# A recommender's attention block: feeding the label's term through eight extra contraction rows in place of a seeded PSUM tile, with label rows gathered by index in place of single-row copies

## The chip, the cores and the metric

The kernel runs on one core of a Trainium2 chip. The metric is the device time of one execution in microseconds (us); the time given is the median of three executions. The profile is one execution recorded by the hardware profiler. In it PE is TensorE's products, PEld its weight loads, DVE is VectorE, ACT is ScalarE, POOL is GpSimd and SP is the SyncE queue, which here only issues DMAs. A name such as L229 is a line of the kernel's file.

## The reference, cut to what matters

For each of 16384 samples there are 69 item ids and one label id. All are rows of one embedding table of 100001 rows of 96 floats. Each item's embedding u meets the label's embedding q in a small attention network; the attended embeddings are summed in ten groups of fields, and three dense layers follow.

```python
u  = emb[batch_user]                     # [B, 69, 96]
ql = emb[batch_label[:, 0]]              # [B, 96]
q  = broadcast of ql over the 69 fields
z  = concatenate([q, u, q - u, q * u], axis=-1)      # [B, 69, 384]
h  = dice(z @ W1 + b1, a1)               # [B, 69, 64], dice(x) = (a (1-p) + p) x, p = sigmoid(x)
att = (h @ W2 + b2) @ W3 + b3            # [B, 69, 1]
pre = where(batch_user < ITEM_NUM, u * att, 0)
pooled = einsum('gf,bfe->bge', window, pre)          # ten groups of fields
x = concatenate([pooled, ql])            # 1056 wide
# three dense layers (200, 80, 1), the first two with batch norm and dice
```

With W1 cut into four pieces of 96 rows, `z @ W1 + b1` is the sum of three terms: `q (W1a + W1c) + b1`, which depends on the sample alone and is called **c** here; `u (W1b - W1c)`, whose weight is called A; and `(q*u) W1d`, whose weight is called Wp. The change is about how c gets into the sum.

## The kernel before

Samples are taken in 32 blocks of 512. A block has 69 chunks of 512 (sample, field) places: 64 chunks hold eight samples with their first 64 fields each, and five tail chunks hold one field of all 512 samples. Chunks are worked on in pairs, 1104 in all; in PSUM the two chunks of a pair lie side by side, the first on partitions 0 to 63, the second on 64 to 127.

The item rows of a chunk come in by four gathers of 128 rows from GpSimd, into one of 14 `u` tiles; TensorE transposes them, VectorE multiplies by q, ScalarE copies the transposed rows:

```python
def gather(dst, index):
    nc.gpsimd.indirect_dma_start(out=dst, out_offset=None, in_=emb,
        in_offset=bass.IndirectOffsetOnAxis(ap=index, axis=0))          # L229

def fetch(i):
    u = upool.tile([P, 8, E], F32, tag="u", name=f"u{i}")                # 14 buffers
    uT, quT = ...                                                        # 5 buffers each
    for j in range(2):
        n, k = chunk(2 * i + j)
        ptr = ps_tr.tile([E, 512], F32, tag="tr", name=f"ptr{i}_{j}")
        for t in range(4):
            gather(u[:, 4 * j + t, :], rows[n][:, 4 * k + t : 4 * k + t + 1])
            nc.tensor.transpose(ptr[:, t * P : (t + 1) * P], u[:, 4 * j + t, :], ident)   # L325
        # VectorE: quT = ptr * q (q broadcast over the 64 fields, or as it is in a tail chunk)   L328, L335
        nc.scalar.copy(uT[:, j, :], ptr)                                 # L336
```

The label rows of block 0 come in by four such gathers. Those of all other blocks are fetched row by row: SP loads 32 labels into registers and issues 32 DMAs of one row each, sixteen times for a block:

```python
def head_gather(n, part):
    ...
    for i, row in enumerate(at):
        nc.sync.dma_start(out=qs[n][p + i : p + i + 1, k, :], in_=emb[bass.ds(row, 1), :])   # L260
```

c is worked out for a whole block, in two layouts (cT with the second half shifted by eight samples, cU without). For each pair a `seed` opens the PSUM tile with a product of zeros, so that later products add to it, and ScalarE writes c over it; `hidden` then adds the two products:

```python
def seed(i):
    ph = ps_h.tile([P, 512], F32, tag="h", name=f"ph{i}")
    nc.tensor.matmul(ph, zrow[:, 0:P], zrow, start=True, stop=False)     # L295, one bf16 row
    # ScalarE copies c into ph: cT spread over 64 fields (L298), cU in tail chunks (L302),
    # or half by half in pairs that mix the two (L307, L312)
    return ph

def hidden(i, ph, uT, quT):
    for w, x, last in [(A, uT, False), (Wp, quT, True)]:
        for j in range(2):
            nc.tensor.matmul(ph[j * H1 : (j + 1) * H1, :], w, x[:, j, :], start=False, stop=last)   # L343
    # sigmoid (L345), scale (L346), product with ph (L347) -> y
```

Further on, four y tiles give a row of attention values (L354, L356), which is turned (L370) and multiplied with the group table (`rw`, L376), and `pool` sums the attended rows into groups (L393, L402). Tail chunks go through L363 and L364, and the dense layers through L423 to L449.

The program is written as a loop over pairs, in which step i seeds pair i-1, pools pair i-8, runs `hidden` for pair i-2 and fetches pair i. A plan hangs the work of block n on the steps near `first`, the pair at which the block begins:

```python
at(first - 24, load ids of block n)         # SP
at(first - 21, map ids to table rows)       # VectorE
at(first - 31 + part, head_gather(n, part)) # part 0 to 15
at(first - 11, head_turn(n))                # transposes q into qT
at(first - 9,  head_row(n))                 # c of the block
at(end + 8 + 4 + s, dense layers of block n, ten steps)   # the last one stores the output from SP
```

Of the kernel before, what the change touches and what calls it, by code (L numbers as in the profile page):

```python
# [28 lines left out]
F32 = mybir.dt.float32  # L31
BF16 = mybir.dt.bfloat16
I32 = mybir.dt.int32
AF = mybir.ActivationFunctionType
ALU = mybir.AluOpType
PSUM = bass.MemoryType.PSUM

P = 128
# [8 lines left out]
FM = 64  # L47
NTAIL = F - FM
NS = BLK // FM
NMAIN = BLK // NS  # L50
NCH = NMAIN + NTAIL
NQ = BLK // P
NT = NCH * 4
NCOL = NT + NQ
NLD = 32
NPAIR = NBLK * NCH // 2
# [8 lines left out]
def rec_kernel(  # L65
    ctx: ExitStack,
    tc: tile.TileContext,
    idx: bass.AP,
    lab: bass.AP,
    emb: bass.AP,  # L70
# [23 lines left out]
    upool = ctx.enter_context(tc.tile_pool(name="upool", bufs=14))  # L94
    tpool = ctx.enter_context(tc.tile_pool(name="tpool", bufs=5))
    hpool = ctx.enter_context(tc.tile_pool(name="hpool", bufs=3))
# [10 lines left out]
    def map_ids(n, ids):  # L107

        rows = ipool.tile([P, NT], I32, tag="rows", name=f"rows{n}")
        nc.vector.scalar_tensor_tensor(rows, ids[:, 0:NT], float(ITEM_NUM), ids[:, 0:NT], ALU.is_ge, ALU.add)  # L110
        return rows

    ids, rows = {0: load_ids(0)}, {}
# [7 lines left out]
    nc.sync.dma_start(out=w1, in_=W1.rearrange("(k e) h -> e k h", e=E))  # L121
    Cq = const.tile([E + 1, 2, H1], F32, name="Cq")
    for i in range(2):
        nc.vector.tensor_add(Cq[0:E, i, :], w1[:, 0, :], w1[:, 2, :])
    nc.sync.dma_start(
        out=Cq[E : E + 1], in_=b1.rearrange("(o q h) -> o q h", o=1, q=1).to_broadcast([1, 2, H1])
    )
    Wp = w1[:, 3, :]
    A = const.tile([E, H1], F32, name="A")
    nc.vector.tensor_sub(A, w1[:, 1, :], w1[:, 2, :])  # L130

    qTs = []
    for i in range(2):
        t = const.tile([E + 1, BLK + NS], F32, name=f"qT{i}")
        nc.vector.memset(t[:, BLK:], 0.0)
        nc.vector.memset(t[E : E + 1, :], 1.0)
        qTs.append(t)
# [60 lines left out]

    zrow = const.tile([1, 512], BF16, name="zrow")
    nc.vector.memset(zrow, 0.0)  # L200

    with tc.tile_pool(name="prep_ps", bufs=1, space=PSUM) as pps:
# [33 lines left out]
    def chunk(c):  # L236

        return divmod(c, NCH)

    def first_head():  # L240

        q = bpool.tile([P, NQ, E], F32, tag="q", name="q0")
        for k in range(NQ):
            gather(q[:, k, :], ids[0][:, NT + k : NT + k + 1])
        return q

    def head_gather(n, part):

        if part == 0:
            qs[n] = bpool.tile([P, NQ, E], F32, tag="q", name=f"q{n}")  # L250
        k, p = divmod(part * NLD, P)
        _, at = nc.values_load_multi_w_load_instructions(  # L252
            lab[n : n + 1, part * NLD : (part + 1) * NLD],
            engines=[mybir.EngineType.SP],
            min_val=0,
            max_val=ITEM_NUM,
            skip_runtime_bounds_check_because="labels are rows of the table",
        )
        for i, row in enumerate(at):
            nc.sync.dma_start(out=qs[n][p + i : p + i + 1, k, :], in_=emb[bass.ds(row, 1), :])  # L260

# [5 lines left out]

    def head_row(n):

        cT = bpool.tile([P, BLK], F32, tag="cT", name=f"cT{n}")  # L270
        pc = ps_x.tile([P, BLK], F32, tag="x", name=f"pc{n}")
        for i in range(2):
            nc.tensor.matmul(
                pc[i * H1 : (i + 1) * H1, :],
                Cq[:, i, :],
                qTs[n % 2][:, i * NS : i * NS + BLK],
                start=True,
                stop=True,
            )
        nc.scalar.copy(cT, pc)  # L280

        cU = bpool.tile([P, BLK], F32, tag="cU", name=f"cU{n}")
        pc = ps_x.tile([P, BLK], F32, tag="x", name=f"pc2_{n}")
        nc.tensor.matmul(pc, Cq.rearrange("e i h -> e (i h)"), qTs[n % 2][:, 0:BLK], start=True, stop=True)
        nc.scalar.copy(cU, pc)
        return cT, cU

    def by_field(ap):

        return ap.rearrange("e (s o) -> e s o", o=1).to_broadcast([ap.shape[0], NS, FM])  # L290

    def seed(i):

        ph = ps_h.tile([P, 512], F32, tag="h", name=f"ph{i}")
        nc.tensor.matmul(ph, zrow[:, 0:P], zrow, start=True, stop=False)  # L295
        (n0, k0), (n1, k1) = chunk(2 * i), chunk(2 * i + 1)
        if n0 == n1 and k1 < NMAIN:
            nc.scalar.copy(  # L298
                ph.rearrange("h (s f) -> h s f", f=FM), by_field(cs[n0][0][:, k0 * NS : (k0 + 1) * NS])
            )  # L300
        elif n0 == n1 and k0 >= NMAIN:
            nc.scalar.copy(ph, cs[n0][1])  # L302
        else:
            for j, (n, k) in enumerate([(n0, k0), (n1, k1)]):
                lo, hi = j * H1, (j + 1) * H1
                if k < NMAIN:
                    nc.scalar.copy(  # L307
                        ph[lo:hi].rearrange("h (s f) -> h s f", f=FM),
                        by_field(cs[n][1][lo:hi, k * NS : (k + 1) * NS]),
                    )  # L310
                else:
                    nc.scalar.copy(ph[lo:hi], cs[n][1][lo:hi, :])  # L312
        return ph

    def fetch(i):

        u = upool.tile([P, 8, E], F32, tag="u", name=f"u{i}")
        uT = tpool.tile([E, 2, 512], F32, tag="uT", name=f"uT{i}")
        quT = tpool.tile([E, 2, 512], F32, tag="quT", name=f"quT{i}")
        for j in range(2):  # L320
            n, k = chunk(2 * i + j)
# [4 lines that stand above are left out]
            q = qTs[n % 2][0:E]  # L326
            if k < NMAIN:
                nc.vector.tensor_tensor(  # L328
                    quT[:, j, :].rearrange("e (s f) -> e s f", f=FM),
                    ptr.rearrange("e (s f) -> e s f", f=FM),  # L330
                    by_field(q[:, k * NS : (k + 1) * NS]),
                    ALU.mult,
                )
            else:
                nc.vector.tensor_tensor(quT[:, j, :], ptr, q[:, 0:BLK], ALU.mult)  # L335
            nc.scalar.copy(uT[:, j, :], ptr)  # L336
        return u, uT, quT

    def hidden(i, ph, uT, quT):

        for w, x, last in [(A, uT, False), (Wp, quT, True)]:
            for j in range(2):
                nc.tensor.matmul(ph[j * H1 : (j + 1) * H1, :], w, x[:, j, :], start=False, stop=last)  # L343
        y = ypool.tile([P, 512], F32, tag="y", name=f"y{i}")
        nc.scalar.activation(y, ph, AF.Sigmoid, scale=S_DICE)  # L345
        nc.scalar.activation(y, y, AF.Identity, bias=a1c, scale=na1c)  # L346
        nc.vector.tensor_mul(y, ph, y)  # L347
        return y
# [10 lines left out]
    def attend_tail(i, j, y, uT):  # L359
# [3 lines left out]
        nc.tensor.matmul(pa, vrep[j * H1 : (j + 1) * H1, :], y[j * H1 : (j + 1) * H1, :], start=True, stop=True)  # L363
        nc.vector.scalar_tensor_tensor(pres[n][:, k - NMAIN, :], pa, bb[0:E], uT[:, j, :], ALU.add, ALU.mult)  # L364

# [78 lines left out]
    def top3(n, x2):  # L444
        p3 = ps_m.tile([1, BLK], F32, tag="m", name=f"p3_{n}")
        nc.tensor.matmul(p3, wf3, x2, start=True, stop=True)
        res = xpool.tile([1, BLK], F32, tag="res", name=f"res{n}")
        nc.vector.tensor_scalar(res, p3, bf3c, None, ALU.add)
# [3 lines left out]

    cs, pooled, pres, x1s, x2s, qs, us, hs, phs, ys, bands, rws, p1s = ({} for _ in range(13))

# [19 lines left out]
    for n in range(NBLK):  # L474
        first, end = n * NCH // 2, ((n + 1) * NCH - 1) // 2
        if n > 0:
            at(first - 24, lambda n=n: ids.__setitem__(n, load_ids(n)))
            at(first - 21, lambda n=n: rows.__setitem__(n, map_ids(n, ids[n])))
            for part in range(BLK // NLD):
                at(first - 31 + part, lambda n=n, part=part: head_gather(n, part))  # L480
            at(first - 11, lambda n=n: head_turn(n, qs.pop(n)))
            at(first - 9, lambda n=n: cs.__setitem__(n, head_row(n)))
        for s, work in enumerate(top_steps(n)):
# [4 lines left out]
    with tc.manual_schedule():  # L488
        head_turn(0, first_head())
        cs[0] = head_row(0)  # L490
        for i in range(NPAIR + POOL_LAG + 16):
            if 0 <= i - 1 < NPAIR:
                phs[i - 1] = seed(i - 1)
            if 0 <= i - POOL_LAG < NPAIR:
# [18 lines left out]
            if 0 <= i - 2 < NPAIR:  # L513
                ys[i - 2] = hidden(i - 2, phs.pop(i - 2), *hs[i - 2])
            if i < NPAIR:
# [58 lines left out]
```

## Time and profile before

| | before |
|---|---|
| time, median of 3 (us) | 11180.09 (11178.86 to 11183.8) |
| span of the profiled execution (us) | 11177.1 |
| mean granted TensorE clock | 0.707 |
| gathers of item rows (POOL, L229) | 8832, mean 951 ns |
| single-row label DMAs (SP, L260) | 15872, 0.4 KB each |
| product of zeros (PE, L295) | 1104, mean 478 ns |
| seeding copies (ACT, L298) | 1008, mean 587 ns |
| DMA traffic | 456.81 MB, mean 41 GB/s |

The page gives for each engine the time in which it executed, as a share of the span. For POOL, the time of an instruction is that of issuing the gather, not of the rows' arrival. A group of instructions is written as line, engine, operation, output and inputs; behind the first bar stand its busy time and the mean of one, behind the second the time the engine was idle just before these instructions, and what ended most of it. "issue" means that the profile shows nothing that the engine waited for.

### The profile page before, as it was taken

What the parts mean: (1) busy time and instruction counts of PE and PEld (TensorE: products, weight loads), DVE (VectorE), ACT (ScalarE), POOL (GpSimd) and SP (SyncE); (2) the same over time, 40 slices, a digit from 0 to 9 for tenths busy, and PEclk for the clock granted to TensorE, in tenths of its full rate; (3) what the DMA queues carried; (4) which work ended last, traced back from release to release, by engine and by line L of the source; (5) the groups of instructions that cost most, each with busy time, mean ns of one, the idle gap of its engine ahead of it and who ended that gap; (6) DMA issues with size and microseconds to landing.
All of it is one profiled execution on the core that took longest, in us unless ns stands there. A gap on an engine that the chain in (4) does not pass through costs nothing.

```text
span 11177.1 us, 157529 instructions
## 1 busy us (share of the span) xinstructions
PE 9700.5 (87%) x41348; PEld 4721.0 (42%) x41348; DVE 3187.3 (29%) x5424; ACT 3760.0 (34%) x6086; POOL 8404.8 (75%) x8842
## 2 busy tenths in 40 slices
PE   6888888888888898888888888888888888988888
PEld 3444444444444444444444444444444344444444
DVE  2222222222222222222222222222222222222222
ACT  2333333333333333333333333333333333333332
POOL 7777777777777777777777777777777777777775
PEclk6767677677776767767777667776677776677767
DMA  2222222222222222222222222222222222222221
GB/s 45 41 41 41 41 41 41 41 41 41 41 41 41 41 41 41 41 42 41 41 41 41 41 41 41 40 41 42 41 41 41 41 42 41 41 41 41 41 40 29
DMA packets 323169, 456.81 MB, mean 41 GB/s; under 512 B 175712, under 2 KB 180864, under 8 KB 322272
## 3 DMA queue, kind: packets, MB, share of 16 engines
q0 software_dynamic: 282752, 434.87, 19.6%
q1 hardware_dynamic: 37886, 10.92, 0.5%
q8 instruction: 333, 5.46, 0.2%
q14 instruction: 564, 4.62, 0.1%
q10 hardware_dynamic: 1634, 0.94, 0.0%
HBM read 446.04 MB, written 0.07 MB: 40 GB/s over the span
## 4 chain that ended last, share of the span: by engine, by line
PE 33%; POOL 32%; issue 16%; DMA 10%; SPq 5%; ACT 2%; DVE 1%; POOLq 0%; ACTq 0%
POOL u L229 32%; PE ph L343 12%; DMA u<-in_emb,rows 10%; PE acc L393 9%; PE p L423 4%; SPq L260 3%; PE ptr L325 3%; PE prow L354 2%; SPq L252 2%; PE ph L295 2%; PE pa L363 1%; ACT y L346 1%; DVE y L347 1%; ACT y L345 1%; PE patt L370 1%
## 5 line engine op out<-in xcount | busy, mean ns | idle before, releaser
L229 POOL DMA_INDIRECT u<-in_emb,rows x8832 | 8400.1, 951 | 2692.9 <-issue 2459.0
L325 PE MATMUL ptr<-ident,u 128*96 128x128 f32 x8832 | 2006.4, 353 | 1189.5 <-DMA u<-in_emb,rows 1172.1
L325 PEld LDWEIGHTS ptr<-ident,u 128*96 128x96 f32 x8832 | 1221.0, 155 | 3053.7 <-DMA u<-in_emb,rows 1526.9
L393 PEld LDWEIGHTS acc<-rw,u 128*96 128x96 f32 x16384 | 2048.5, 217 | 531.8 <-issue 531.2
L393 PE MATMUL acc<-rw,u 128*96 128x20 f32 x16384 | 2160.4, 282 | 1.8 <-DVE rw L376 1.3
L336 ACT COPY uT<-ptr 96x512 f32<-96x512 f32 x2208 | 1283.4, 581 | 2207.0 <-DVE quT L328 2039.4
L347 DVE TENSOR_TENSOR y<-ph,y 128x512 f32<-128x512 f32 x1104 | 763.5, 692 | 4394.8 <-ACT y L346 4292.3
L345 ACT ACTIVATE y<-ph 128x512 f32<-128x512 f32 x1104 | 659.1, 597 | 3754.1 <-PE ph L343 3753.9
L343 PE MATMUL ph<-uT,A 96*64 96x512 f32 x4416 | 1793.5, 904 | 0.0
L343 PE MATMUL ph<-quT,w 96*64 96x512 f32 x4416 | 1671.9, 847 | 0.0
L328 DVE TENSOR_TENSOR quT<-ptr,qT 96x512 f32<-96x512 f32 x2048 | 1348.9, 679 | 611.5 <-PE ptr L325 607.0
L402 DVE COPY pooled<-acc 96x160 f32<-96x160 f32 x1008 | 433.3, 430 | 2189.9 <-PE acc L393 2184.4
L346 ACT ACTIVATE y<-y,a1c,na1c 128x512 f32<-128x512 f32 x1104 | 897.2, 813 | 36.6
L343 PEld LDWEIGHTS ph<-quT,w 96*64 96x64 f32 x4416 | 442.8, 194 | 1074.9 <-issue 1074.9
L298 ACT COPY ph<-cT 128x512 f32<-128x512 f32 x1008 | 591.3, 587 | 498.2 <-PE ph L295 497.8
L295 PE MATMUL ph<-zrow 1*128 1x512 bf16 x1104 | 527.6, 478 | 193.4 <-DVE y L347 191.7
L423 PE MATMUL p<-pooled,wf 96*100 96x512 f32 x1280 | 659.4, 660 | 1.2 <-DVE x L427 0.8
L343 PEld LDWEIGHTS ph<-uT,A 96*64 96x64 f32 x4416 | 282.6, 177 | 550.0 <-issue 464.8
L354 PE MATMUL prow<-y,v 128*32 128x512 f32 x2208 | 455.2, 909 | 0.0
L356 ACT COPY row<-prow 128x512 f32<-128x512 f32 x276 | 161.5, 585 | 628.4 <-PE prow L354 622.9
L423 PEld LDWEIGHTS p<-pooled,wf 96*100 96x100 f32 x1280 | 232.2, 190 | 287.7 <-issue 285.5
L423 PE MATMUL p<-pre,V 96*100 96x512 f32 x640 | 314.6, 625 | 0.0
(71 smaller groups left out, 2318.5 us busy)
## 6 DMA issues: line engine op xcount, KB each, us to landing
q<-in_emb SPq DMA_DIRECT2D x15872, 0.4 KB
u<-in_emb,rows POOLq DMA_INDIRECT x8832
ids<-in_idx SPq DMA_DIRECT2D x32, 140.0 KB
wf<-in_Wf ACTq DMA_DIRECT2D x1, 825.0 KB
out<-res SPq DMA_DIRECT2D x32, 2.0 KB
w<-in_W SPq DMA_DIRECT2D x1, 96.0 KB
q<-in_emb,ids POOLq DMA_INDIRECT x4
wf<-in_Wf ACTq DMA_DIRECT2D x1, 62.5 KB
```

What stands on the lines that cost most here:

```text
L229: nc.gpsimd.indirect_dma_start(out=dst, out_offset=None, in_=emb, in_offset=bass.IndirectOffsetOnAxis(ap=index, axis=0),)
L295: nc.tensor.matmul(ph, zrow[:, 0:P], zrow, start=True, stop=False)
L325: nc.tensor.transpose(ptr[:, t * P : (t + 1) * P], u[:, 4 * j + t, :], ident)
L328: nc.vector.tensor_tensor(quT[:, j, :].rearrange("e (s f) -> e s f", f=FM), ptr.rearrange("e (s f) -> e s f", f=FM), by_field(q[:, k * NS ...
L336: nc.scalar.copy(uT[:, j, :], ptr)
L343: nc.tensor.matmul(ph[j * H1 : (j + 1) * H1, :], w, x[:, j, :], start=False, stop=last)
L345: nc.scalar.activation(y, ph, AF.Sigmoid, scale=S_DICE)
L346: nc.scalar.activation(y, y, AF.Identity, bias=a1c, scale=na1c)
L347: nc.vector.tensor_mul(y, ph, y)
L354: nc.tensor.matmul(pr[32 * k : 32 * (k + 1), :], v2, y, start=True, stop=True)
L393: nc.tensor.matmul(pa[:, j, 2 * t : 2 * t + 2, :].rearrange("e n g -> e (n g)"), u[:, 4 * j + t, :], rw[:, i % 4, j, t, :], start=True, st ...
L423: nc.tensor.matmul(p1, w[:, h * DH : (h + 1) * DH], x, start=(k == 0), stop=(k == KTOP - 1))
```

## The change

c is no longer written into PSUM. The contraction of the first product grows from 96 rows to 104: the moving operand gets eight constant rows that say which of the chunk's eight samples a column belongs to, and the weights get the eight samples' rows of c below A. There are then 64 weight tiles (one for each chunk of a block), held in two tiles of 32, and the rows of c are put there by small DMAs from SP. In tail chunks, where each column is another sample, c comes from a product of its own with Cq. The product of zeros and the seeding copies go away.

The label rows of every block are gathered by GpSimd with four gathers, as block 0's were; the single-row DMAs of SP go away. The gathers stand at first - 14. The mapped ids are written in place, the uT tiles become five constant tiles, quT has four buffers in place of five, and the output row shares a buffer with another tile.

What it is for: to take the opening product and the copies off TensorE and ScalarE.

The diff, with the removed bodies of `seed`, `head_row` and the old `head_gather` (all shown above) and small declarations cut:

```diff
     def map_ids(n, ids):
-        rows = ipool.tile([P, NT], I32, tag="rows", name=f"rows{n}")
-        nc.vector.scalar_tensor_tensor(rows, ids[:, 0:NT], float(ITEM_NUM), ids[:, 0:NT], ALU.is_ge, ALU.add)
+        rows = ids[:, 0:NT]
+        nc.vector.scalar_tensor_tensor(rows, rows, float(ITEM_NUM), rows, ALU.is_ge, ALU.add)
         return rows
 ...
-    A = const.tile([E, H1], F32, name="A")
-    nc.vector.tensor_sub(A, w1[:, 1, :], w1[:, 2, :])
+    A = [const.tile([E + NS, HM, H1], F32, name=f"A{h}") for h in range(2)]
+    nc.vector.tensor_sub(A[0][0:E, 0, :], w1[:, 1, :], w1[:, 2, :])
+    for h in range(2):
+        nc.vector.tensor_copy(
+            A[h][0:E, 1 - h :, :], A[0][0:E, 0:1, :].to_broadcast([E, HM - 1 + h, H1])
+        )
+    uTs = [const.tile([E + NS, 2, 512], F32, name=f"uT{i}") for i in range(5)]
+    for t in uTs:
+        for j in range(2):
+            nc.vector.tensor_copy(
+                t[E : E + NS, j, :].rearrange("e (s f) -> e s f", f=FM), by_field(ident[E : E + NS, E : E + NS])
+            )
 ...
+    def head_gather(n):
+        q = bpool.tile([P, NQ, E], F32, tag="q", name=f"q{n}")
         for k in range(NQ):
-            gather(q[:, k, :], ids[0][:, NT + k : NT + k + 1])
+            gather(q[:, k, :], ids[n][:, NT + k : NT + k + 1])
         return q
 ...
+    def head_rows(n):
+        c = bpool.tile([P, NQ, H1], F32, tag="c", name=f"c{n}")
+        pc = ps_x.tile([P, NQ, H1], F32, tag="x", name=f"pc{n}")
+        for k in range(NQ):
+            nc.tensor.matmul(pc[:, k, :], qTs[n % 2][:, k * P : (k + 1) * P], Cq, start=True, stop=True)
+        nc.scalar.copy(c, pc)
+        return c
+
+    def head_weights(c, h):
+        for s in range(NS):
+            for k in range(NQ // 2):
+                nc.sync.dma_start(
+                    out=A[h][E + s : E + s + 1, k * HM // 2 : (k + 1) * HM // 2, :],
+                    in_=c[s::NS, h * NQ // 2 + k, :],
+                )
 ...
-    def hidden(i, ph, uT, quT):
-        for w, x, last in [(A, uT, False), (Wp, quT, True)]:
-            for j in range(2):
-                nc.tensor.matmul(ph[j * H1 : (j + 1) * H1, :], w, x[:, j, :], start=False, stop=last)
+    def hidden(i, uT, quT):
+        ph = ps_h.tile([P, 512], F32, tag="h", name=f"ph{i}")
+        places = [chunk(2 * i + j) for j in range(2)]
+        sums = [ph[j * H1 : (j + 1) * H1, :] for j in range(2)]
+        for (n, k), p in zip(places, sums):
+            if k >= NMAIN:
+                nc.tensor.matmul(p, Cq, qTs[n % 2], start=True, stop=False)
+        for j, ((n, k), p) in enumerate(zip(places, sums)):
+            if k < NMAIN:
+                nc.tensor.matmul(p, A[k // HM][:, k % HM, :], uT[:, j, :], start=True, stop=False)
+            else:
+                nc.tensor.matmul(p, A[0][0:E, 0, :], uT[0:E, j, :], start=False, stop=False)
+        for j, p in enumerate(sums):
+            nc.tensor.matmul(p, Wp, quT[:, j, :], start=False, stop=True)
 ...
-            for part in range(BLK // NLD):
-                at(first - 31 + part, lambda n=n, part=part: head_gather(n, part))
+            at(first - 14, lambda n=n: qs.__setitem__(n, head_gather(n)))
             at(first - 11, lambda n=n: head_turn(n, qs.pop(n)))
-            at(first - 9, lambda n=n: cs.__setitem__(n, head_row(n)))
+            at(first - 9, lambda n=n: cs.__setitem__(n, head_rows(n)))
+            at(first - 7, lambda n=n: head_weights(cs[n], 0))
+            at(first + 4, lambda n=n: head_weights(cs.pop(n), 1))
```

More of the change, by code (lines that the diff above doesn't have):

```diff
@@ L31 @@
 F32 = mybir.dt.float32
-BF16 = mybir.dt.bfloat16
 I32 = mybir.dt.int32
@@ L50 @@
 NMAIN = BLK // NS
+HM = NMAIN // 2
 NCH = NMAIN + NTAIL
@@ L54 @@
 NCOL = NT + NQ
-NLD = 32
 NPAIR = NBLK * NCH // 2
@@ L68, in rec_kernel @@
     idx: bass.AP,
-    lab: bass.AP,
     emb: bass.AP,
@@ L94, in rec_kernel @@
     upool = ctx.enter_context(tc.tile_pool(name="upool", bufs=14))
-    tpool = ctx.enter_context(tc.tile_pool(name="tpool", bufs=5))
+    tpool = ctx.enter_context(tc.tile_pool(name="tpool", bufs=4))
     hpool = ctx.enter_context(tc.tile_pool(name="hpool", bufs=3))
@@ L107, in map_ids, with by_field @@
     def map_ids(n, ids):
-        rows = ipool.tile([P, NT], I32, tag="rows", name=f"rows{n}")
-        nc.vector.scalar_tensor_tensor(rows, ids[:, 0:NT], float(ITEM_NUM), ids[:, 0:NT], ALU.is_ge, ALU.add)
-        return rows
+        rows = ids[:, 0:NT]
+        nc.vector.scalar_tensor_tensor(rows, rows, float(ITEM_NUM), rows, ALU.is_ge, ALU.add)
+        return rows
+    def by_field(ap):
+        return ap.rearrange("e (s o) -> e s o", o=1).to_broadcast([ap.shape[0], NS, FM])
     ids, rows = {0: load_ids(0)}, {}
@@ L121, in rec_kernel @@
     nc.sync.dma_start(out=w1, in_=W1.rearrange("(k e) h -> e k h", e=E))
[L122 to L127, printed above, removed]
-    Wp = w1[:, 3, :]
-    A = const.tile([E, H1], F32, name="A")
-    nc.vector.tensor_sub(A, w1[:, 1, :], w1[:, 2, :])
+    Cq = const.tile([E + 1, H1], F32, name="Cq")
+    nc.vector.tensor_add(Cq[0:E], w1[:, 0, :], w1[:, 2, :])
+    nc.sync.dma_start(out=Cq[E : E + 1], in_=b1.rearrange("(o h) -> o h", o=1))
+    Wp = w1[:, 3, :]
+    A = [const.tile([E + NS, HM, H1], F32, name=f"A{h}") for h in range(2)]
[10 more added lines that the diff above has]
+            )
     qTs = []
     for i in range(2):
-        t = const.tile([E + 1, BLK + NS], F32, name=f"qT{i}")
-        nc.vector.memset(t[:, BLK:], 0.0)
+        t = const.tile([E + 1, BLK], F32, name=f"qT{i}")
         nc.vector.memset(t[E : E + 1, :], 1.0)
@@ L197, in rec_kernel @@
     nc.vector.tensor_scalar_mul(sbf2, bf2c, S_BN)
-    zrow = const.tile([1, 512], BF16, name="zrow")
-    nc.vector.memset(zrow, 0.0)
     with tc.tile_pool(name="prep_ps", bufs=1, space=PSUM) as pps:
@@ L238, in chunk @@
         return divmod(c, NCH)
-    def first_head():
-        q = bpool.tile([P, NQ, E], F32, tag="q", name="q0")
+    def head_gather(n):
+        q = bpool.tile([P, NQ, E], F32, tag="q", name=f"q{n}")
         for k in range(NQ):
-            gather(q[:, k, :], ids[0][:, NT + k : NT + k + 1])
+            gather(q[:, k, :], ids[n][:, NT + k : NT + k + 1])
         return q
[L247 to L260, printed above, removed]
     def head_turn(n, q):
@@ L266, in head_turn @@
         nc.vector.tensor_copy(qTs[n % 2][0:E, 0:BLK], pq)
[L268 to L313, printed above, removed]
+    def head_rows(n):
[5 more added lines that the diff above has]
+        return c
@@ L315, in fetch @@
+    def head_weights(c, h):
[5 more added lines that the diff above has]
+                )
     def fetch(i):
         u = upool.tile([P, 8, E], F32, tag="u", name=f"u{i}")
-        uT = tpool.tile([E, 2, 512], F32, tag="uT", name=f"uT{i}")
+        uT = uTs[i % len(uTs)]
         quT = tpool.tile([E, 2, 512], F32, tag="quT", name=f"quT{i}")
@@ L335, in fetch @@
                 nc.vector.tensor_tensor(quT[:, j, :], ptr, q[:, 0:BLK], ALU.mult)
-            nc.scalar.copy(uT[:, j, :], ptr)
+            nc.scalar.copy(uT[0:E, j, :], ptr)
         return u, uT, quT
-    def hidden(i, ph, uT, quT):
-        for w, x, last in [(A, uT, False), (Wp, quT, True)]:
-            for j in range(2):
-                nc.tensor.matmul(ph[j * H1 : (j + 1) * H1, :], w, x[:, j, :], start=False, stop=last)
+    def hidden(i, uT, quT):
[12 more added lines that the diff above has]
+            nc.tensor.matmul(p, Wp, quT[:, j, :], start=False, stop=True)
         y = ypool.tile([P, 512], F32, tag="y", name=f"y{i}")
@@ L363, in attend_tail @@
         nc.tensor.matmul(pa, vrep[j * H1 : (j + 1) * H1, :], y[j * H1 : (j + 1) * H1, :], start=True, stop=True)
-        nc.vector.scalar_tensor_tensor(pres[n][:, k - NMAIN, :], pa, bb[0:E], uT[:, j, :], ALU.add, ALU.mult)
+        nc.vector.scalar_tensor_tensor(pres[n][:, k - NMAIN, :], pa, bb[0:E], uT[0:E, j, :], ALU.add, ALU.mult)
     def spread(b, row):
@@ L446, in top3 @@
         nc.tensor.matmul(p3, wf3, x2, start=True, stop=True)
-        res = xpool.tile([1, BLK], F32, tag="res", name=f"res{n}")
+        res = xpool.tile([DH, BLK], F32, tag="g1", name=f"res{n}")[0:1]
         nc.vector.tensor_scalar(res, p3, bf3c, None, ALU.add)
@@ L451, in rec_kernel @@
     out_v = out.rearrange("(n b) o -> n (o b)", n=NBLK)
-    cs, pooled, pres, x1s, x2s, qs, us, hs, phs, ys, bands, rws, p1s = ({} for _ in range(13))
+    cs, pooled, pres, x1s, x2s, qs, us, hs, ys, bands, rws, p1s = ({} for _ in range(12))
     def top_steps(n):
@@ L488, in rec_kernel @@
     with tc.manual_schedule():
-        head_turn(0, first_head())
-        cs[0] = head_row(0)
+        qs[0] = head_gather(0)
+        head_turn(0, qs.pop(0))
+        cs[0] = head_rows(0)
+        for h in range(2):
+            head_weights(cs[0], h)
         for i in range(NPAIR + POOL_LAG + 16):
-            if 0 <= i - 1 < NPAIR:
-                phs[i - 1] = seed(i - 1)
             if 0 <= i - POOL_LAG < NPAIR:
@@ L513, in rec_kernel @@
             if 0 <= i - 2 < NPAIR:
-                ys[i - 2] = hidden(i - 2, phs.pop(i - 2), *hs[i - 2])
+                ys[i - 2] = hidden(i - 2, *hs[i - 2])
             if i < NPAIR:
@@ L535 @@
     tail = user[:, :, FM:].reshape(NBLK, NQ, P, NTAIL).transpose(0, 2, 3, 1).reshape(NBLK, P, NTAIL * NQ)
+    labels = x["batch_label"].reshape(NBLK, NQ, P).transpose(0, 2, 1)
     window = x["window"]
@@ L539 @@
         wtile[n, :, n, :] = window[:, :FM].T
-    labels = x["batch_label"].reshape(NBLK, NQ, P).transpose(0, 2, 1)
     arrays = {
         "idx": np.concatenate([main, tail, labels], axis=2),
-        "lab": x["batch_label"].reshape(NBLK, BLK),
         "emb": np.concatenate([x["emb"], np.zeros((1, E), np.float32)], axis=0),
```

## The prediction

> **What bounds the kernel now.** I read four views in this order: the page's busy shares, the view of the gather's source line, the waits, and the timeline around single gathers.
>
> The busy shares alone mislead. TensorE is the busiest engine and GpSimd, which issues the gathers, seems to have a quarter of the span to spare:
>
> ```profile
> PE 9700.5 (87%) x41348; PEld 4721.0 (42%) x41348; DVE 3187.3 (29%) x5424; ACT 3760.0 (34%) x6086; POOL 8404.8 (75%) x8842
> ```
>
> The view of the source line that gathers gives duration (least, median, greatest, in ns) and the first and last start:
>
> ```profile
> L229 POOL DMA_INDIRECT u<-in_emb,rows x8832: 940/944/1582, 8.6 to 11100.4; - x197
> ```
>
> The waits say what the missing quarter is (after the arrow: what ended the idle time, then the microseconds in all, the times, the longest single one):
>
> ```profile
> POOL u L229 <- issue: 2459.0, 8065, 0.3
> ...
> POOL u L229 <- PE ptr L325: 105.8, 347, 0.3
> POOL u L229 <- DMA u<-in_emb,rows: 101.9, 334, 0.3
> ```
>
> Every one of the 8832 gathers is preceded by about 0.3 us of idle time, and the longest is 0.3 us too, whichever engine is put down as the releaser. So GpSimd never waits for anybody: 0.3 us is the price of starting a gather, and one named after PE or DMA is the same gap with an event near it. Listing all gathers from the timeline, I find no gap over 0.32 us. The first gather starts at 8.6 us and the last at 11100.4, so the period is (11100.4 - 8.6) / 8831 = **1.256 us**, and the time is a sum of three pieces: 8.6 us of head, 8831 x 1.256 = 11091.8 us of gathers, 76.7 us of tail after the last gather starts. That is the whole span of 11177.1.
>
> The groups by cost say the same from TensorE's side (columns: busy us, mean ns | idle us before, and what ended it):
>
> ```profile
> L229 POOL DMA_INDIRECT u<-in_emb,rows x8832 | 8400.1, 951 | 2692.9 <-issue 2459.0
> L325 PE MATMUL ptr<-ident,u 128*96 128x128 f32 x8832 | 2006.4, 353 | 1189.5 <-DMA u<-in_emb,rows 1172.1
> ...
> L343 PE MATMUL ph<-uT,A 96*64 96x512 f32 x4416 | 1793.5, 904 | 0.0
> ...
> L298 ACT COPY ph<-cT 128x512 f32<-128x512 f32 x1008 | 591.3, 587 | 498.2 <-PE ph L295 497.8
> L295 PE MATMUL ph<-zrow 1*128 1x512 bf16 x1104 | 527.6, 478 | 193.4 <-DVE y L347 191.7
> ```
>
> TensorE stands still for 1172 us in all before a transpose, waiting for rows that a gather has not landed yet. TensorE follows GpSimd; GpSimd follows nothing.
>
> **What the Trainium skill says, and whether the trace agrees.** (1) "DMA: Bandwidth & Descriptors", section "SWDGE vs HWDGE vs iDMA": for a DMA issued from GpSimd, cores of GpSimd compute the descriptors in software; one issued from SP gets them from hardware. The trace agrees as far as it can: each gather holds GpSimd for 0.944 us in the middle, and SP's row fetches leave GpSimd's line alone. (2) The same page, "Issuing engines are not separate DMA queues": issuing from another engine saves only the sequencer's time, which it calls usually small. Here that time is the bound, so the saving is all that counts. (3) "SBUF — State Buffer", "Who interferes with whom": a VectorE instruction with two SBUF inputs shares a port with GpSimd, and the later one waits. The timeline agrees: the gather that starts during the product rw<-R,w takes 1.38 us, those beside it 0.95 and 0.94:
>
> ```profile
> 5187.81 0.95 POOL L229 DMA_INDIRECT u<-in_emb,rows  x1 [0.30 <-issue]
> ...
> 5188.80 0.83 DVE L376 TENSOR_TENSOR rw<-R,w 128x640 f32<-128x640 f32 x1
> ...
> 5189.06 1.38 POOL L229 DMA_INDIRECT u<-in_emb,rows  x1 [0.30 <-issue]
> ```
>
> (4) "TensorE: Matmul & The Clock Gate", "Step-by-step: what each phase is for": a product takes the time of its streamed columns and a weight load that of its weight columns; the number of contraction rows doesn't enter. The trace shows it for 97 against 96 rows (843 ns for pc<-qT,Cq, 847 for ph<-quT,w, both means), so I count 104 rows at no extra time.
>
> **The change, part by part.**
>
> *Label fetch.* Removed from SP: 31 x 512 = 15872 single-row DMAs, at about 0.54 us each (a stretch of 288 took 156.55 us): 8.6 ms of SP time that nobody on the bounding path waited for. Added to GpSimd: four gathers for each of the 31 blocks after the first (the first block's four were gathers already), 31 x 4 = 124. At 1.256 us each, start price included, they cost **124 x 1.256 = +155.7 us**, and all of it is on the path, because GpSimd has no gap to put them in.
>
> *Opening product and seed.* Removed: 1104 one-row bf16 products (527.6 us busy, 193.4 us of idle before them) on TensorE, and on ScalarE 1008 seeding copies (591.3 us) and the 128 smaller or tail ones (37.7 + 18.7 + 18.6 us). The two wide c products and two copies of each block become four narrow products and one copy. Added: for each tail chunk a product with Cq, 5 x 32 = 160, each in two passes as the 4416 records for 2208 products show: 320 passes at 1793.5 / 4416 = 0.41 us, 130 us. TensorE comes out some 500 to 600 us lighter, ScalarE 650 us lighter. On the path: **0**. TensorE will wait that much longer for rows.
>
> *Weights with c in them.* 32 small DMAs for each block (eight rows, two pieces, two halves), 1024 in all, from SP, which has been freed. They are issued 9 loop steps before the first half is read and some 14 before the second. A loop step is eight gathers, 10.05 us, so some 90 and 140 us for 16 DMAs which, at 0.54 us of issue, take 9 us: **0**.
>
> *Prologue.* VectorE fills the two A tiles (1984 and 2048 elements a partition) and the indicator rows of five uT tiles (10 copies of 512). At 690 ns for 512 elements, as the y product shows, that is 2.7 + 2.8 + 6.9 = 12 us of SBUF-to-SBUF work while the first gathers run. By (3) some can collide; in this trace the 216 gathers over 0.96 us lost 67 us in all, 0.3 each, so I put **+4 us** for a handful. TensorE starts some 10 us later, but GpSimd runs into 14 u tiles ahead of it, and TensorE has the slack to catch up.
>
> *Tail.* After the last gather: two seeds fewer, two to three Cq products more: **0**, give or take a few microseconds.
>
> Sum: 11180.1 + 155.7 + 4 = **11340 us**, 1.4% slower.
>
> **The rivals.**
>
> A. *TensorE is as good as the bound*, and losing 500 us or more lets everything move up. For it: 87% busy, and ph<-uT,A the largest share of the chain after the gather. It would give about 11180 - 527.6 - 193.4 + 155.7 = 10615 us. Against it: if TensorE held GpSimd back, it would be by keeping u tiles, and gaps beyond 0.32 us would have to appear. There is none.
>
> B. *The 124 gathers are hidden* in GpSimd's idle quarter: 11180. Against it: that quarter is the start price, and it comes again with each gather.
>
> C. *A new wait takes over*: weights that land late, or SP stuck in order behind the output store (it waits up to 350 us for its result). Then TensorE would stop at block starts, u tiles would run out, and GpSimd would show gaps. With 10 us a block it gives +320 us, 11660. Against it: the store is awaited some six steps ahead of the first half's DMAs, and VectorE has its result at that step.
>
> D. *The single-row DMAs slow the gathers now*, and without them each gets cheaper. The stretch after the last of them (10571 us) tells: 420 gathers at 1.2535 us against 1.2560 over all. But the time lost in gathers over 0.96 us is 5.1 ns a gather there and 7.5 over all, which is the same 2.5 ns; the base is unchanged. At most it would take 8956 x 2.5 ns = 22 us off.
>
> **Range and chances.** The +155.7 is a count times a period that stays within 1.2546 to 1.2601 in every stretch of 1000 us, so it is good to 1 us. Collisions with VectorE cost 67 us now, and a shifted phase could change that by a third, 22 us; head and tail may be off by 8 us each. D pulls down, the prologue and a little of C up. So **11315 to 11370**. The 2% line is 11403.7: only C reaches it (0.05); faster by 2% needs A (0.01).
>
> **What would show it.** The gather's row should read 8832 again, with q<-in_emb,ids at 128, period 1.25 to 1.26, idle before each at 0.3 us at the longest. TensorE's wait for u<-in_emb,rows should grow by hundreds of microseconds, and its busy time fall, with the span longer all the same. SP's 15872 DMAs should be gone. I am wrong if GpSimd shows gaps of microseconds (C), if the mean gather leaves 945 to 956 ns, or if the period shrinks.

## The result and the profile after

The changed kernel takes **11338.75 us** (median of 4, 11329.85 to 11350.31) against 11181.65 for the kernel before (the three executions given above and one more): a ratio of 1.0141, interval 1.0124 to 1.0159. It is slower by 157 us, though TensorE and ScalarE have less to do.

The busy shares of the page after:

```profile
PE 9172.4 (81%) x40628; PEld 4609.5 (41%) x40628; DVE 3201.5 (28%) x5432; ACT 3153.1 (28%) x4918; POOL 8534.0 (75%) x8966
```

TensorE has lost 528 us of busy time and ScalarE 607. GpSimd has gained 129 us and its share is still 75%, in a longer span. Its source line, with duration and first and last start, now shows both kinds of gather:

```profile
L237 POOL DMA_INDIRECT u<-in_emb,ids x8832: 940/944/1594, 9.2 to 11266.0; - x197
...
L237 POOL DMA_INDIRECT q<-in_emb,ids x128: 940/944/1557, 3.4 to 10783.5; - x128
```

There are 8960 gathers, with the same median of 944 ns. The waits of GpSimd after, each with its longest in the last column:

```profile
POOL u L237 <- issue: 2500.5, 8205, 0.3
...
POOL u L237 <- DMA u<-in_emb,ids: 109.1, 358, 0.3
...
POOL u L237 <- PE ptr L289: 58.5, 192, 0.3
```

Again no idle time over 0.3 us after the first gather: GpSimd goes from gather to gather from one end to the other. The groups of TensorE by shape show what became of the time it was relieved of:

```profile
L289 PE MATMUL ptr<-ident,u 128*96 128x128 f32 x8832 | 2125.6, 340 | 2123.8 <-DMA u<-in_emb,ids 2097.1 <-ACT y L320 10.8 <-DVE quT L292 1.0
...
L317 PE MATMUL ph<-quT,w 96*64 96x512 f32 x4416 | 1664.7, 826 | 0.0
L313 PE MATMUL ph<-uT,A 104*64 104x512 f32 x4096 | 1664.2, 892 | 0.0
...
L313 PEld LDWEIGHTS ph<-uT,A 104*64 104x64 f32 x4096 | 265.1, 176 | 451.2 <-issue 430.9 <-DMA A<-c 1.9
```

Before its transposes TensorE now waits 2097 us for gathered rows, 925 more than before. The product over 104 rows takes 892 ns, against 904 over 96 rows before. The granted clock was higher, though (0.729, before 0.707), and the product with quT, which has 96 rows in both kernels, went from 847 to 826 ns; measured against it, the eight rows cost about 1%. The weights that carry c made it wait 1.9 us in the whole run.

### The profile page after: what moved, and what is told of

It reads as the page before. It is cut to its first block, busy times and chain, and to the rows that moved or that the text cites. A ratio compares the mean times of both kernels' runs of the same rounds, so it can differ in the third digit from the quotient of the medians.

```text
span 11348.5 us, 107380 instructions
## 1 busy us (share of the span) xinstructions
PE 9172.4 (81%) x40628; PEld 4609.5 (41%) x40628; DVE 3201.5 (28%) x5432; ACT 3153.1 (28%) x4918; POOL 8534.0 (75%) x8966
## 4 chain that ended last, share of the span: by engine, by line
POOL 48%; issue 22%; PE 19%; DMA 11%; DVE 0%; POOLq 0%; ACT 0%; SPq 0%; ACTq 0%; DVEq 0%
POOL u L237 47%; DMA u<-in_emb,ids 11%; PE acc L367 4%; PE p L397 3%; PE ph L313 3%; PE ph L317 3%; PE ptr L289 2%; PE prow L328 2%; POOL q L237 1%; PE pa L337 1%; PE ph L310 1%; PE ph L315 0%; PE patt L344 0%; PE pc L266 0%; PE pq L258 0%
## 5 line engine op out<-in xcount | busy, mean ns | idle before, releaser
L237 POOL DMA_INDIRECT u<-in_emb,ids x8832 | 8411.8, 952 | 2691.6 <-issue 2500.5
L289 PE MATMUL ptr<-ident,u 128*96 128x128 f32 x8832 | 2125.6, 340 | 2123.8 <-DMA u<-in_emb,ids 2097.1
L289 PEld LDWEIGHTS ptr<-ident,u 128*96 128x96 f32 x8832 | 1135.1, 145 | 4170.3 <-DMA u<-in_emb,ids 2534.9
L367 PEld LDWEIGHTS acc<-rw,u 128*96 128x96 f32 x16384 | 2143.8, 221 | 216.3 <-issue 181.3
L367 PE MATMUL acc<-rw,u 128*96 128x20 f32 x16384 | 2083.5, 277 | 1.8 <-DVE rw L350 1.3
L292 DVE TENSOR_TENSOR quT<-ptr,qT 96x512 f32<-96x512 f32 x2048 | 1371.8, 681 | 1319.7 <-PE ptr L289 1316.8
L313 PE MATMUL ph<-uT,A 104*64 104x512 f32 x4096 | 1664.2, 892 | 0.0
L313 PEld LDWEIGHTS ph<-uT,A 104*64 104x64 f32 x4096 | 265.1, 176 | 451.2 <-issue 430.9
L350 DVE TENSOR_TENSOR rw<-R,w 128x640 f32<-128x640 f32 x276 | 229.3, 831 | 9.5
L344 PE MATMUL patt<-ident,row 128*128 128x128 f32 x1104 | 217.1, 330 | 14.6 <-DVE pre L338 14.6
```

Of the source, the lines that this page charges most:

```text
L292: nc.vector.tensor_tensor(quT[:, j, :].rearrange("e (s f) -> e s f", f=FM), ptr.rearrange("e (s f) -> e s f", f=FM), by_field(q[:, k * NS ...
L313: nc.tensor.matmul(p, A[k // HM][:, k % HM, :], uT[:, j, :], start=True, stop=False)
L367: nc.tensor.matmul(pa[:, j, 2 * t : 2 * t + 2, :].rearrange("e n g -> e (n g)"), u[:, 4 * j + t, :], rw[:, i % 4, j, t, :], start=True, st ...
```

## The experiments

The theory: GpSimd's gathers alone set the time, so the label gathers cost their count times the period, 1.256 us, and the new way of c is worth nothing. The rivals are those of the prediction.

### One part alone: the label rows

Edit to the kernel before: the label gathers of the change, and nothing else.

```diff
...
-            for part in range(BLK // NLD):
-                at(first - 31 + part, lambda n=n, part=part: head_gather(n, part))
+            at(first - 14, lambda n=n: qs.__setitem__(n, head_gather(n)))
```

> The kernel before with only the label rows gathered by GpSimd, taken again for the same reason. Where the kernel before takes about 11180 us: 11336 us (11320 to 11352), ratio 1.014, the same as the changed kernel; rival B 11180. Where the kernel before takes some 15400 us: the ratio 0.87 of the first try again.

Measured: 11345.22 us (4 runs) against 11185.98 for the kernel before on this chip, ratio 1.0144, interval 1.0128 to 1.0159. GpSimd now gathers the label rows too, and again none of its waits is over 0.3 us:

```profile
L228 POOL DMA_INDIRECT q<-in_emb,ids x128: 940/944/1165, 3.3 to 10782.3; - x128
...
POOL u L228 <- issue: 2369.1, 7774, 0.3
```

This is the whole of the change's slowdown, with the zero product and the seeds still in place. Rival B falls: gathers do not hide in the idle quarter. Rival A falls too, in one direction: taking the c work off TensorE on top of this, which is the changed kernel with its 1.0141, changes nothing outside the intervals.

### One part alone: the way of c

First try: the changed kernel with SP's single-row label DMAs put back.

> The same kernel as the first one with single-row label DMAs and the new way of c, taken again because on the chip of the first try the kernel before itself took 15458 us, with GpSimd waiting thousands of microseconds for TensorE. Where the kernel before takes about 11180 us, the theory (gathers alone) says 11165 to 11200 us and a longest gap of 0.32 us before a gather; rival A anything below 11150; rival C above 11200 with longer gaps. Where the kernel before takes some 15400 us again, the ratio of the first try, 1.11, should come back.

Measured: 11207.95 us (20 runs), ratio 1.0019, interval 1.0012 to 1.0026: 22 us slower, though TensorE is busy for only 8375.8 us. So rival A gets nothing, but the theory's range is missed by 8 us, and what was named as the sign of rival C is there: above 11200, with a longer gap. GpSimd's timeline shows one single gap, and the SP and TensorE timelines of the same run where it comes from:

```profile
309.39 0.94 POOL L239 DMA_INDIRECT u<-in_emb,ids  x1 [0.30 <-issue]
329.96 0.94 POOL L239 DMA_INDIRECT u<-in_emb,ids  x1 [19.63 <-PE acc L384]
```

```profile
43.46 120.94 SPq L270 DMA_DIRECT2D q<-in_emb  x224
164.46 0.38 SPq L106 DMA_DIRECT2D ids<-in_idx  x1
169.58 156.06 SPq L270 DMA_DIRECT2D q<-in_emb  x288
342.93 42.42 SPq L291 DMA_DIRECT2D A<-c  x32
```

```profile
326.83 0.42 PE L275 MATMUL pq<-ident,q 128*96 128x128 f32 x1 [70.57 <-DMA q<-in_emb]
```

SP begins block 1's 512 row DMAs at 43 us, behind the weights of block 0, and ends at 326. The transposes of these rows stand next in TensorE's program, and it waits 70.57 us for the last of them; the u tiles run out; GpSimd stops for 19.63 us. In the kernel before, SP begins the same rows 27 us earlier:

```profile
16.93 120.66 SPq L260 DMA_DIRECT2D q<-in_emb  x224
```

```profile
300.87 0.42 PE L265 MATMUL pq<-ident,q 128*96 128x128 f32 x1 [46.39 <-DMA q<-in_emb]
```

There TensorE stands for 46.39 us at this place, and GpSimd has no gap: the u tiles carry it over a wait of 46 us, but not over one of 71. The wait of 19.63 us belongs to the mixture of the two versions, which puts label rows and weights into one queue. It is not in the changed kernel, where the longest gap is 0.3 us.

Second try: the same kernel with the row DMAs planned twelve steps earlier.

```diff
...
-                at(first - 31 + part, lambda n=n, part=part: head_gather(n, part))
+                at(max(0, first - 43 + part), lambda n=n, part=part: head_gather(n, part))
```

> The new way of c with single-row label DMAs from SP, these now planned twelve loop steps earlier (at first - 43 and on, in place of first - 31), so that SP's waits for c and for the weight tiles no longer make a block's label rows late. Theory (gathers alone): the one gap of 19.6 us that the same kernel showed before block 1 is gone, none over 0.32 us is left, and the time is that of the kernel before plus 0 to 8 us: 11180 to 11194, ratio 0.999 to 1.001. If the way of c itself cost 22 us (rival C), it stays at 11208, ratio 1.002. If the freed TensorE time counts (rival A), it falls below 11150.

Measured: 11787.88 us (5 runs), ratio 1.0536, interval 1.0522 to 1.0551. The remedy was wrong, and no test of c. The waits show why:

```profile
DVE ids L112 <- DMA ids<-in_idx: 2561.3, 32, 175.3
...
PEld acc L384 <- DVE pooled L393: 1668.4, 24, 167.0
```

The ids of a block now stand behind 512 row DMAs in SP's order, where they stood behind 224. VectorE waits up to 175 us for them, with the rest of its program behind; TensorE waits up to 167 us for VectorE, and GpSimd waited 646.2 us in gaps put down to the product acc.

Third try, which takes the label fetch out of the question: the changed kernel with block 0's label rows used for every block. It leaves out the fetch of the other 15872 rows; all else is done as often as in the changed kernel.

```diff
...
-            at(first - 14, lambda n=n: qs.__setitem__(n, head_gather(n)))
-            at(first - 11, lambda n=n: head_turn(n, qs.pop(n)))
+            at(first - 11, lambda n=n: head_turn(n, qs[0]))
```

> The changed kernel without the label fetch of blocks 1 to 31 (block 0's label rows serve all blocks; the fetch of 15872 rows is left out), taken again for the same reason as the others. Theory: 11339 - 155.7 = 11183 us (11170 to 11195). Rival D (single-row DMAs slow the gathers): faster than the kernel with early single-row DMAs by up to 22 us, with a shorter median gather; by the theory the two agree within 6 us.

Measured: 11197.26 us (13 runs), ratio to the kernel before 1.0008, interval 1.0000 to 1.0017. No gap before a gather is over 0.32 us:

```profile
POOL u L237 <- issue: 2456.6, 8063, 0.3
```

The new way of c is worth nothing: 0 to 19 us lost, none won, with TensorE busy for 9077.2 us in place of 9700.5. Rival D falls as well: this kernel has neither label gathers nor single-row DMAs, and is not faster than the kernel before, which has 15872 of them. The time alone would not settle that, since its gathers lost 19 us more beside VectorE, which could hide a gain of up to 22; the even part in the table below does: 11031.7 us against 11030.4. The theory's point value was 14 us too low, and its range ended 2 us too low; the table says where these are.

### Gathers beside VectorE

Edit to the changed kernel: three VectorE products get their second operand from PSUM. (The axes of rw are put into the order in which PSUM holds w; pool reads it accordingly.)

```diff
-        w = rpool.tile([P, 4, 2, 4], F32, tag="w", name=f"w{b}")
+        w = pt[:, :, :, 0:2]                       # in PSUM, over the turned rows themselves
...
-        nc.scalar.activation(g1, g1, AF.Identity, bias=af1c[h], scale=naf1c[h])
-        nc.vector.tensor_mul(x1, x1, g1)
+        nc.scalar.activation(p1, g1, AF.Identity, bias=af1c[h], scale=naf1c[h])   # p1 is in PSUM
+        nc.vector.tensor_mul(x1, x1, p1)           # and the same for g2 and p2
```

> The changed kernel with one operand of three VectorE products moved from SBUF to PSUM: w of rw<-R,w is written in place over the transposed attention rows in PSUM, and the gates g of the dense layers are written over their own sums in PSUM. Same arithmetic, same gathers. If long gathers come from VectorE holding the port for a second SBUF operand, the 75 us that gathers over 0.96 us lost at these products vanish and the time falls to 11339 - 70 = 11269 us (11258 to 11285), ratio to before 1.008, with the spread between executions (20 us for the changed kernel) shrinking. If long gathers come from something else that only happens at the same time (the products of TensorE, a DMA), 11339 stays.

Measured: 11280.85 us (5 runs, 11279.63 to 11286.56), ratio to before 1.0087, interval 1.0073 to 1.0100. Against the 1.0141 of the changed kernel this is some 60 us less, where 70 were expected. The source line's durations (least, median, greatest), to be compared with those after:

```profile
L237 POOL DMA_INDIRECT u<-in_emb,ids x8832: 940/944/1179, 9.1 to 11191.7; - x197
```

The greatest falls from 1594 to 1179 ns. Of 8960 gathers 38 are over 0.96 us, against 217 before the edit, and most of the 38 lie beside the mapping of ids and the tail weights, which were left as they were. In the changed kernel's timeline 145 of the 389 gathers that ran beside rw<-R,w were over 0.96 us, after the edit 2 of 375. Beside the products that have an operand in PSUM in both kernels they were rare before it too: 2 of 2479 at quT<-ptr,qT, 2 of 1442 at y<-ph,y. So it is the second SBUF operand, and not VectorE's work as such. This is what the Trainium skill says in "SBUF — State Buffer", "Who interferes with whom", of two SBUF inputs; the runs add its price, 78.9 us in all before the edit and 4.8 after it.

### Two other chips, on which GpSimd is not the bound

Seven runs fell on two chips on which the kernel before took 15458 us (four of the runs) and 15427 us (three). Three of these kernels were run again on chips where it took 11186 to 11187 us, as told above; of the other three there are times from those two chips alone. One of them is a further try to separate c from the label rows:

```diff
...
-                nc.sync.dma_start(
+                nc.scalar.dma_start(                # ScalarE's queue in place of SP's
                     out=A[h][E + s : E + s + 1, k * HM // 2 : (k + 1) * HM // 2, :],
```

The second is the changed kernel with a second set of label gathers into an unread tile, the third the kernel before with the PSUM operands of the last section.

> The changed kernel with the label rows of blocks 1 to 31 copied row by row from SP again, so that only the way of c into the sum is changed. Theory (GpSimd's gathers alone set the time): 8836 gathers as in the kernel before, so 11180 us, plus the few us of the longer prologue: 11165 to 11200, ratio to before 0.999 to 1.002, although TensorE is some 500 us less busy. Rival A (TensorE's and ScalarE's work is partly on the path): the freed 500 to 700 us show, in full 10460 us, in part anything below 11150. Rival C (the weights that carry c make TensorE wait): above 11200, with gaps over 0.32 us between gathers.

> The kernel before with only the label rows changed: four GpSimd gathers a block, seeds and zero product kept. Theory: 124 more gathers at 1.256 us, 11180 + 155.7 = 11336 us (11320 to 11352), the same as the changed kernel within its own spread of 10 us. Rival A: slower than the changed kernel by what the lighter TensorE is worth there. Rival B (gathers hide in GpSimd's idle quarter): 11180.

> The changed kernel without the label fetch of blocks 1 to 31: block 0's label rows are used for every block (this leaves out the fetch of 15872 label rows). 8836 gathers and no single-row DMAs from SP. Theory: 11339 - 155.7 = 11183 us (11165 to 11200), equal to the kernel with single-row DMAs within 10 us. Rival D (single-row DMAs slow the gathers): faster than that kernel by up to 22 us, with a shorter median gather.

> The changed kernel with each block's label rows gathered twice, first into a tile nobody reads: 128 more gathers, 9088 in all. Theory: 11339 + 128 x 1.256 = 11500 us (11485 to 11515), the same price a gather as the change paid. Rival B: 11339. A wait in the way of the first 124 (rather than their own cost) would make the second 128 cost clearly more or less than 1.25 us each.

> The changed kernel with each block's label rows gathered twice (first into a tile nobody reads), 9088 gathers, taken again on a chip where the kernel before takes its 11180 us. Theory: 11339 + 128 x 1.25 = 11499 us (11485 to 11515), ratio to before 1.0275 to 1.030. Rival B (gathers hide in the idle quarter): 11339.

> The new way of c with single-row label DMAs from SP at their old steps, and the 32 small DMAs a block that put c into the weights issued from ScalarE's queue, so that they no longer stand in SP's order between label rows and ids. If the gap of 19.6 us (weights and label rows both on SP) and the loss of 600 us (label rows earlier on SP) came from SP's one queue in order, no gap over 0.32 us is left and the time is that of the kernel before plus 0 to 20 us, according to how much gathers lose to VectorE: 11183 to 11206. If the way of c is what makes TensorE late, gaps stay. Rival A (freed TensorE time counts): below 11150.

> The kernel before with only the three VectorE products' second operands moved to PSUM (w of rw<-R,w and the gates of the dense layers). Its gathers over 0.96 us lost 67 us in all, 63 of them beside these products. Theory (gathers alone, and the port lengthens them): 11186 - 62 = 11124 us (11112 to 11136), ratio 0.993 to 0.996, gathers over 0.96 us down to a few dozen. If the port doesn't matter for this kernel: 11186.

Measured there, against the kernel before on the same chip:

| kernel | us | ratio, interval |
|---|---|---|
| changed, single-row DMAs from SP | 17166.09 | 1.1115 (1.1089 to 1.1142) |
| the same, weights issued from ScalarE | 16566.79 | 1.0732 (1.0702 to 1.0762) |
| before, no second SBUF operand | 15521.89 | 1.0052 (1.0035 to 1.0070) |
| before, label gathers | 13440.71 | 0.8706 (0.8688 to 0.8725) |
| changed, label rows gathered twice | 13353.99; 13363.51 | 0.8653 (0.8631 to 0.8674); 0.8666 (0.8637 to 0.8696) |
| changed, block 0's label rows only | 13017.27 | 0.8434 (0.8412 to 0.8456) |

None of the times fits the theory, and the waits show that its premise is gone. From the kernel before without second SBUF operands, on one of those chips:

```profile
PEld acc L391 <- issue: 3559.1, 1039, 42.9
POOL u L229 <- PE acc L391: 3185.5, 240, 92.6
...
ACT y L345 <- remote: 2880.9, 281, 29.5
```

GpSimd waits up to 92.6 us at a time for TensorE to give back u tiles, and TensorE stands up to 42.9 us with nothing in the profile that it waits for. The page's mean of a gather there is 944 ns, so the edit has shortened them as on the other chips, and the time doesn't fall (ratio 1.0052): GpSimd is not what it depends on. What the runs show is an order: kernels with 15872 single-row DMAs on SP take 15.4 to 17.2 ms, those without 13.0 to 13.4. What stops TensorE was not found, and single-row DMAs as its cause are not shown. The granted clock is not enough of a cause: with block 0's label rows only it was 0.720 there against 0.740, and the time 13017 us against 11197. These runs decide nothing about 1.0141, and they leave three questions unanswered: the price of the second 128 gathers, whether weights from ScalarE's queue remove the gap of 19.63 us, and whether the kernel before gains from the PSUM operands. That last one would be the candidate to beat both kernels; no run shows that it does.

## Why the prediction was right, point by point

The timelines of all gathers, added up for the profiled executions. "Long" is what gathers over 0.96 us took beyond 0.944; the even part is what is left between the first and the last start.

| kernel | gathers | even part | long | one gap | head and tail | span |
|---|---|---|---|---|---|---|
| before | 8836 | 11030.4 | 66.6 | | 80.1 | 11177.1 |
| changed, one label block | 8836 | 11031.7 | 85.8 | | 85.0 | 11202.5 |
| changed, SP label rows | 8836 | 11030.4 | 67.4 | 19.3 | 80.3 | 11197.4 |
| changed | 8960 | 11183.8 | 78.9 | | 85.8 | 11348.5 |
| before, label gathers | 8960 | 11184.2 | 77.7 | | 84.4 | 11346.3 |
| changed, no second SBUF operand | 8960 | 11183.5 | 4.8 | | 89.4 | 11277.7 |

In these six programs the even part goes with the number of gathers alone: 11030 to 11032 for 8836, 11184 for 8960.

- **Label fetch, +155.7.** Right. The even part grows by 153.4 us from before to after, 1.24 us a gather. The 1.256 used for it held the losses to VectorE as well.
- **Opening product and seed, 0 on the path.** Right. ScalarE's busy time fell by 607 us (650 said), TensorE's by 528 (500 to 600 said), and TensorE's wait for rows grew by 925. The agreement on TensorE proves little: its busy time is not the amount of work alone, for the same 40628 instructions took 8375.8 us with SP's label rows and 9172.4 in the changed kernel. The 104 rows cost about 1% more than 96, on TensorE, off the path.
- **Weights, 0.** Right: 1.9 us of waiting.
- **Prologue, +4.** Its size was off. The two A tiles took 3.40 us and not 5.5, the ten copies 3.55 and not 6.9, and the gathers of the first 60 us lost 1.5 us to VectorE, 0.9 more than before. These copies read one SBUF operand, so point (3) of the prediction, which is about two, is no ground for expecting collisions with them; the gathers beside them were lengthened all the same.
- **Tail, 0.** It is 5.8 us longer than before (82.5 against 76.7 from the last gather's start to the end), within the few said. Why stays open.
- **Collisions.** The range allowed a third, 22 us; they grew by 12.3 in the profiled run, and by 19.2 in the one with one label block. The even part, the long gathers and the two ends together, +153.4 + 12.3 + 5.7, are the 171.4 us by which the profiled span grew; the profiled execution is the slowest of the four. The forecast sum was 160, and the medians grew by 157: that 11340 lies 1 us from the median is luck, as the four executions spread over 20 us.
- **Rivals.** A, B and D are refuted as told. (The share of the chain that the prediction gives to ph<-uT,A for A is that of L343, which holds the product with quT as well.) C doesn't happen in the changed kernel; it does as soon as the label rows stay on SP beside the weights.

## What to carry to other kernels

An engine with short, equal gaps before each of its instructions is full, whatever its busy share says (here 0.3 us before each of 8960 gathers, at 75% busy): look at the longest gap before an instruction, and multiply count by period. Work moved onto such an engine costs its full price (124 gathers, 153 us); work taken off the others buys waiting time. Before a transfer is moved from one in-order queue to another, look at what else stands in that queue and who waits behind it: here the same row DMAs cost nothing, 20 us or 600 us according to what stood around them.

## What was not expected

VectorE products with both operands in SBUF cost GpSimd's gathers 60 to 80 us a run, and moving one operand to PSUM gave back some 60 us of time in a kernel that is otherwise unchanged. The amount differs from one program to the next; that the phase of the two engines decides it was not shown. Nor was it shown that it makes the spread between executions: 20 us with these products in the changed kernel and 7 without them, but 5 in four executions of the kernel before, which has them. And the same programs on two other chips had another bound, with the label gathers 13% faster there instead of 1.4% slower: a change that moves work between queues is worth measuring on more than one chip.
